# Layer 0 of a four-layer network: VectorE in source order in step one, products a tile later and half of them on POOL, operand blocks of 112 partitions instead of 128

## Chip, cores and metric

The kernel runs on one core of a Trainium2 chip. Its metric is the time on the device of one execution, in microseconds (us); a comparison takes the median over several runs. A profiled execution is one more run, taken with the hardware profiler.

The engines go by the names of the profile: PE is TensorE's matmul and PEld its weight load, DVE is VectorE, ACT ScalarE, POOL GpSimd, SP the sync engine, which here only issues transfers. ACT and POOL issue transfers too, each from its own queue.

## The reference, cut to what matters

Four layers work on an image batch of 8 x 56 x 56 x 192 in float32, each as `x = x + layer(groupnorm(x))`. Only layer 0 is touched by the change:

```python
p = silu(x @ p_w.T + p_b)            # 192 -> 576 channels
q = silu(x @ q_w.T + q_b)
v = silu(x @ v_w.T + v_b)
qv = q * v
a1 = rpe_mlp1(position) * decay      # 111 lags x 576 channels
a2 = rpe_mlp2(position) * decay
o1 = toeplitz(qv along w, a1)        # one 56 x 56 Toeplitz matrix per channel
o2 = toeplitz(qv along h, a2)
out = (p * (o1 + o2)) @ o_w.T + o_b
```

For one channel with the image X (56 rows by 56 columns) this means o1 + o2 = X T1 + T2 X, where T1 and T2 are that channel's Toeplitz matrices. Layer 1 is windowed attention, layer 2 a convolution with four exponential scans, layer 3 a 7 x 7 depthwise convolution and an MLP.

## The kernel before

Activations lie with channels on partitions: a tile of an image is 128 partitions (64 channels twice, once for the upper and once for the lower half of the image) by 3 groups of 64 channels by NH = 1568 pixels. Layer 0 has two stages.

**Step one** (the `with` block from L1321) runs over the 8 images. `layer0_load` (L353) brings an image in from POOL's queue, into one of two buffers. `layer0_in` (L358) takes the statistics of the group norm (four `gn_piece` of three instructions each), finishes them with two small matmuls and a square root, and writes the normed image `xn` (L371), on VectorE throughout. `layer0_qv` (L374) then runs over 14 tiles of two image rows in each half (112 pixels twice). For each half `n` of the 576 channels it makes 24 matmuls into two PSUM tiles (there are four, and they fill PSUM), adds the bias while it empties PSUM (L393, VectorE), takes the Silu in place (L394, ACT) and multiplies q and v into the tile `qv` (L395, VectorE). Both image halves of a tile are then stored by SP to two DRAM tensors: `left`, with an image row per row (L398, one transfer per half), and `right`, transposed, with an image column per row (L403, two transfers per half). Both stores write runs of 256 bytes, 64 channels of one pixel.

Between tiles, in `between[i]`, other work is called: `toeplitz_rows` builds the table of lags in the first image and later the 112 rows of Toeplitz matrices in DRAM, issued by ACT (L296); `build_bias_mask` and `layer1_weights` prepare layer 1; `layer0_in` of the next image is called as a whole after tile 4. The scheduler of the framework orders all engines' instructions itself, by its own estimate of times, and may place an instruction well before its place in the source.

**The mix** (`layer0_mix`, L523) runs over images and nine groups of 64 channels. `layer0_block` (L410) has SP load two operand blocks for a group, `lt` and `rt`, each 128 partitions by 3584 elements: 64 rows of qv and 64 rows of Toeplitz matrix in alternation. Only 56 rows of each are needed. The other eight are zero rows on the Toeplitz side, written in step one (L301, from a row of zeros called `none`), and on the qv side whatever rows follow. There are two buffers for each block (pool `raws`), and the first two pairs are loaded already during step one. `layer0_operand` (L422) copies eight channels of a block at a time into matmul order, `lc` on POOL and `rc` on VectorE and ACT in turn (L425). `layer0_products` (L428) makes one matmul per channel (L433), which sums over the partitions, so over X T1 and T2 X together. The results are copied out, transposed, gated with p and projected (`layer0_gate`); those steps are woven between the products by count. When an image's gate is done its result `x1` is stored (L538, two transfers from 64 partitions each) and a further image loaded (L528), both by SP.

Of the kernel before, what the change touches and what calls it, by code (L numbers as in the profile page):

```python
# [18 lines left out]
NT = H * W  # L19
# [43 lines left out]
NH = NT // 2  # L63
NTH = NH // TT
# [25 lines left out]
def kernel(ctx: ExitStack, tc: tile.TileContext, a: dict, out: bass.AP):  # L90
# [45 lines left out]
    none = dram.tile([QR], F32, name="none")  # L136
    left, right = (dram.tile([(nimg * W + 64) * NSUB, QR], F32, name=n) for n in ("left", "right"))
    qv_row = lambda b, s: (b * NSUB + s) * W
    toep_row = lambda s: nimg * NSUB * W + 64 * s
    x1 = [dram.tile([C, NT], F32, name=f"x1_{b}") for b in range(nimg)]  # L140
# [86 lines left out]
    def toeplitz_rows(psum, pool, rows):  # L227
# [130 lines left out]
    def layer0_in(b, x, pool, psum):  # L358

        sc, sh = scsh[:, 0, b:b + 1], scsh[:, 1, b:b + 1]  # L360
        st = pool.tile([128, 3, NTH, 6], F32, name="gh_st")
        for t in range(NTH):
            gn_piece(st, x, t)
        mv = pool.tile([128, 1, 2], F32, name="gh_mv")
        gn_aggregate(st, mv[:, 0])
        run(gn_finish(mv, sc, sh, pool, psum, "qv"))
        xn = pool.tile([128, 3, NH], F32, name="xn0")
        n = NH if b else TT
        for t in range(NH // n):
            ts = bass.ts(t, n)  # L370
            nc.vector.tensor_scalar(xn[:, :, ts], x[:, :, ts], sc, sh, ALU.mult, ALU.add)  # L371
        return xn

    def layer0_qv(b, xn, pool, psum, w_qv, b_qv, between):  # L374

        lv, rv = (
            z[qv_row(b, 0):qv_row(b, 0) + NSUB * W].rearrange("(s h) (w d) -> s h w d", h=W, d=64) for z in (left, right)
        )
        for i in range(PH):
            qv = pool.tile([2 * W, 2, D1], F32, name="qv", bufs=3)  # L380
            for n in range(2):
                ns = slice(n * D1 // 2, (n + 1) * D1 // 2)
                ps = [psum.tile([2 * W, 2, 512], F32, name=f"qv{s}", tag="qv") for s in range(2)]
                for which in range(2):
                    for j in range(3):
                        for s in range(2):
                            nc.tensor.matmul(  # L387
                                ps[s][:, which, 0:D1 // 2], xn[64 * s:64 * s + 64, j, bass.ts(i, 2 * W)],
                                w_qv[64 * s:64 * s + 64, j, which, ns], start=(j == 0), stop=(j == 2),
                            )  # L390
                for s in range(2):
                    act = pool.tile([2 * W, 2, D1 // 2], F32, name="act", bufs=4)
                    nc.vector.tensor_tensor(act, ps[s][:, :, 0:D1 // 2], b_qv[:, :, ns], ALU.add)  # L393
                    nc.scalar.activation(act, act, AF.Silu)  # L394
                    nc.vector.tensor_tensor(qv[:, s, ns], act[:, 0], act[:, 1], ALU.mult)  # L395
            for s in range(2):
                h0 = H // 2 * s + 2 * i
                nc.sync.dma_start(  # L398
                    lv[:, h0:h0 + 2].rearrange("s h w d -> (h w) s d"),
                    qv[:, s].rearrange("t (s d) -> t s d", d=64),  # L400
                )
                for r in range(2):
                    nc.sync.dma_start(  # L403
                        rv[:, :, h0 + r].rearrange("s w d -> w s d"),
                        qv[r * W:(r + 1) * W, s].rearrange("w (s d) -> w s d", d=64),
                    )
            for step in between[i]:
                step()

    def layer0_block(b, s, raws):  # L410
# [3 lines left out]
        rows_qv, rows_t = qv_row(b, s), toep_row(s)  # L414
        for t, z, even, odd in ((raw[0], left, rows_t, rows_qv), (raw[1], right, rows_qv, rows_t)):
            one = z[even:even + 64]
            nc.sync.dma_start(
                t, bass.AP(one.tensor, one.offset, [[QR, 64], [(odd - even) * QR, 2], [1, QR]]),
            )
        return raw  # L420

    def layer0_operand(copy, raw, name, bufs, d0, nu, pool):  # L422

        c = pool.tile([128, 2, 8, W], F32, name=name, bufs=bufs)
        copy(c[:, 0:nu], raw.rearrange("p (w u d) -> p u d w", u=nu, d=64 // nu)[:, :, d0:d0 + 8])  # L425
# [896 lines left out]
    with ExitStack() as st:  # L1322
# [3 lines left out]
        b_qv = pool.tile([2 * W, 2, D1], F32, name="b_qv", bufs=1)  # L1326
        nc.scalar.dma_start(b_qv.rearrange("p a d -> p (a d)"), a["b_qv"].partition_broadcast(2 * W))
        tz = st.enter_context(tc.tile_pool(reuse_waits="tile", name="tz", bufs=2))
        x = layer0_load(0, pool)
        xn = layer0_in(0, x, pool, psum)  # L1330
# [8 lines left out]
        for b in range(nimg):  # L1339

            between = {i: [lambda i=i: pop(rows, 2 if i % 3 == 1 else 1)] for i in range(PH)}
            if b == 0:
                for i in range(PH):
# [340 lines left out]
```

## Time and profile before

| what | value |
|---|---|
| time, median of 3 runs (lowest to highest) | 5769.45 us (5760.73 to 5771.72) |
| profiled execution, time / span from first to last instruction | 5770.6 us / 5768.8 us |
| start to first L387 matmul | 28.6 us |
| step one, first to last L387 matmul | 28.6 to 847.1 us: PE busy 731.3, VectorE 598.0, ACT 320.4, POOL 42.3 of 818.5 us, DMA share 0.85 |
| mix of layer 0, to its last L433 product | 847.1 to 2052.5 us: PE busy 1083.7, VectorE 652.8, ACT 469.8, POOL 556.7 of 1205.4 us, DMA share 0.67 |
| layers 1 to 3 and what is left of layer 0 | 2052.5 to 5768.8 us |

The busy time of a stretch is the time in which an engine had an instruction of the program under way. The DMA share is the time that packets took on 16 DMA engines, as a part of the stretch. A wait is put down to the instruction that released it last.

### The profile page before, as it was taken

To read this page: it belongs to the slowest core of one execution; us is meant where nothing else is said; L and a number is where in the kernel's file an instruction comes from. 1 tells how busy PE (TensorE), PEld (TensorE's weight loads), DVE (VectorE), ACT (ScalarE), POOL (GpSimd) and SP (SyncE) were. 2 spreads that over 40 slices of the span, in tenths; PEclk is the share of its full clock that TensorE was granted. 3 is DMA by queue.
4 is the path that set the end of the run, shared out by engine and by line. 5 is a ranking of instruction groups with operands and counts; after the bars stand their busy time and mean duration, and the time that the engine had idled before them with its cause. 6 is when DMAs were issued, how large, how long until landed. Compare 5 with 4: busy or idle time off the path is not lost. (4 is left out here: it accounts for less than half of the span.)

```text
span 5768.8 us, 116138 instructions
## 1 busy us (share of the span) xinstructions
PE 5181.2 (90%) x50342; PEld 3376.1 (59%) x50342; DVE 3336.5 (58%) x4710; ACT 2169.1 (38%) x2908; POOL 1420.2 (25%) x1107
## 2 busy tenths in 40 slices
PE   6898998999899979999997989999788798999999
PEld 4568765666666645555554657676344597444444
DVE  5777774555555546566665868888778202433331
ACT  2333443333333423333332004555476400433333
POOL 2100004444444424433342013333101101100100
PEclk8999999999999989999998989999899899999999
DMA  6888986776677633222222866666687598212211
GB/s 179 204 211 216 206 182 258 264 264 258 247 262 264 222 92 82 69 75 76 69 65 76 260 235 218 227 232 209 160 232 215 222 328 295 78 62 77 76 41 26
DMA packets 721922, 1013.94 MB, mean 176 GB/s; under 512 B 486376, under 2 KB 645444, under 8 KB 694644
## 3 DMA queue, kind: packets, MB, share of 16 engines
q1 hardware_dynamic: 706352, 940.12, 52.4%
q0 software_dynamic: 8512, 40.62, 2.1%
q10 hardware_dynamic: 6548, 25.78, 1.4%
q8 instruction: 396, 6.49, 0.5%
q14 instruction: 114, 0.93, 0.0%
HBM read 676.92 MB, written 345.97 MB: 177 GB/s over the span
## 5 line engine op out<-in xcount | busy, mean ns | idle before, releaser
L387 PE MATMUL qv<-w_qv_sb,xn 64*112 64x288 f32 x5376 | 711.3, 421 | 48.6 <-DVE act L393 45.4
L425 POOL COPY lc<-lt 128x896 f32<-128x896 f32 (+1 forms) x320 | 552.5, 1751 | 640.9 <-PE op L433 543.1
L387 PEld LDWEIGHTS qv<-w_qv_sb,xn 64*112 64x112 f32 x5376 | 558.5, 182 | 195.5 <-DVE act L393 58.1
L394 ACT ACTIVATE act<-act 112x576 f32<-112x576 f32 x448 | 300.6, 683 | 466.8 <-DVE act L393 427.4
L433 PE MATMUL op<-rc,lc 128*56 128x56 f32 x9216 | 339.1, 221 | 102.1 <-POOL lc L425 64.9
L433 PEld LDWEIGHTS op<-rc,lc 128*56 128x56 f32 x9216 | 307.8, 135 | 177.9 <-POOL lc L425 103.5
L1289 PE MATMUL ph<-y,w_sb 64*128 64x392 f32 x2304 | 397.7, 497 | 6.5 <-ACT hid L1293 6.5
L1300 PE MATMUL po<-hid,w_sb 128*64 128x392 f32 x2304 | 386.3, 494 | 0.0
L393 DVE TENSOR_TENSOR act<-qv,b_qv 112x576 f32<-112x576 f32 x448 | 320.7, 752 | 92.7 <-PE qv L387 92.4
L1307 DVE TENSOR_TENSOR x<-x,z 128x392 f32<-128x392 f32 x96 | 67.0, 698 | 524.2 <-ACT z L1305 524.2
L425 ACT COPY rc<-rt 128x896 f32<-128x896 f32 (+1 forms) x160 | 256.3, 1606 | 249.7 <-PE op L433 227.2
L805 PE MATMUL qk_ps<-xr,wg 64*96 64x392 f32 x1536 | 334.2, 538 | 1.8 <-DVE xr L752 1.7
L1016 PE MATMUL cv<-zc,wt 128*128 128x224 f32 x1536 | 313.6, 356 | 24.2 <-DMA zc<-pd 24.2
L1016 PEld LDWEIGHTS cv<-zc,wt 128*128 128x128 f32 x1536 | 291.0, 190 | 67.5 <-issue 51.2
L1289 PEld LDWEIGHTS ph<-y,w_sb 64*128 64x128 f32 x2304 | 220.0, 188 | 175.9 <-issue 25.5
L445 PE MATMUL pj<-xn,w_p_sb 64*128 64x392 f32 x1536 | 309.8, 511 | 12.4 <-DVE xn L533 8.2
L1190 PE MATMUL cps<-zc,wt 128*128 128x224 f32 x1536 | 300.2, 356 | 18.2 <-DMA zc<-zd 16.8
L1190 PEld LDWEIGHTS cps<-zc,wt 128*128 128x128 f32 x1536 | 289.6, 189 | 28.7 <-issue 21.3
L466 PE MATMUL y<-pp,w_o_sb 128*64 128x392 f32 x1536 | 285.9, 501 | 4.8 <-DVE x L474 4.1
L459 DVE TENSOR_TENSOR pp<-pp,ot 128x784 f32<-128x784 f32 x128 | 124.2, 970 | 284.8 <-ACT pp L450 272.9
L1300 PEld LDWEIGHTS po<-hid,w_sb 128*64 128x64 f32 x2304 | 162.7, 137 | 213.8 <-issue 213.8
L1031 POOL TENSOR_TENSOR rows<-rows,loc 128x896 f32<-128x896 f32 x96 | 220.8, 2300 | 261.7 <-ACT rows L1027 201.9
(233 smaller groups left out, 8895.1 us busy)
## 6 DMA issues: line engine op xcount, KB each, us to landing
lt<-left SPq DMA_DIRECT2D x72, 1792.0 KB
rt<-right SPq DMA_DIRECT2D x72, 1792.0 KB
left<-qv SPq DMA_DIRECT2D x224, 252.0 KB
right<-qv SPq DMA_DIRECT2D x448, 126.0 KB
wt<-in_band_dram SPq DMA_DIRECT2D x23, 2048.0 KB
wt<-in_band_dram SPq DMA_DIRECT2D x11, 4096.0 KB
zc<-pd SPq DMA_DIRECT2D x187, 232.0 KB
pd<-pt SPq DMA_DIRECT2D x7, 5568.0 KB
```

Source lines behind the costliest of these rows:

```text
L387: nc.tensor.matmul(ps[s][:, which, 0:D1 // 2], xn[64 * s:64 * s + 64, j, bass.ts(i, 2 * W)], w_qv[64 * s:64 * s + 64, j, which, ns], start ...
L393: nc.vector.tensor_tensor(act, ps[s][:, :, 0:D1 // 2], b_qv[:, :, ns], ALU.add)
L394: nc.scalar.activation(act, act, AF.Silu)
L425: copy(c[:, 0:nu], raw.rearrange("p (w u d) -> p u d w", u=nu, d=64 // nu)[:, :, d0:d0 + 8])
L433: nc.tensor.matmul(op[64 * u:64 * u + W, i, :], lc[:, u, i], rc[:, u, i], start=True, stop=True)
L445: nc.tensor.matmul(ps[0:M, s, 0:TT], w_p[64 * s:64 * s + 64, j, d0:d0 + M], xn[64 * s:64 * s + 64, j, ts], start=(j == 0), stop=(j == 2),)
L466: nc.tensor.matmul(y[64 * s:64 * s + 64], w_o[0:M, c, 64 * j:64 * j + 64], pp[0:M, s], start=(c == gated[0][0]), stop=(c == gated[-1][0]),)
L805: nc.tensor.matmul(in_pairs(ps[s]), wg[64 * s:64 * s + 64, j, c0:c0 + HC], in_slots(xr[64 * s:64 * s + 64], (3 * g + j) * GW), start=(j == ...
L1016: nc.tensor.matmul(dst, wt[:, c4 + i, 128 * q:128 * q + 128], zc[:, :, c4 + i, q:q + NPAIR], start=(q == 0), stop=(q == 1),)
L1190: nc.tensor.matmul(dst.rearrange("p (b n) -> p b n", n=NPAIR), wt[:, c4 + i, q * OP:(q + 1) * OP], zc[:, :, c4 + i, q:q + NPAIR], start=(q ...
L1289: nc.tensor.matmul(ps[:, s, 0:TT], w0[64 * s:64 * s + 64, j, m * 128:(m + 1) * 128], y[64 * s:64 * s + 64, j, ts], start=(j == 0), stop=(j ...
L1300: nc.tensor.matmul(ps[64 * s:64 * s + 64], w1[:, m, 64 * j:64 * j + 64], hid[:, m, s], start=(m == 0), stop=(m == 5),)
```

## The change

In step one:

- VectorE's instructions are issued in the order of the source (`manual_schedule` for DVE alone); the other engines stay with the scheduler.
- The first part of the lag table is called before the first image's statistics. `layer0_in` becomes a generator: one statistics piece, or one part of the finish, or two of the four pieces of `xn`, is called after each of tiles 3 to 12 of the image before. The scaling to `xn` goes to POOL for all images but the first.
- The product of q and v is put off by half a tile (`later`): it is issued after the next half's additions. The product of the upper image half stays on VectorE, that of the lower half goes to POOL. The stores follow it; they are the same transfers, in number, size and (for `left`) place.

In the operand blocks: the Toeplitz rows no longer get zero rows behind them, and the row of zeros goes. `right` has its Toeplitz rows first and its qv rows behind. A block is loaded on 112 partitions, 56 rows of qv and 56 of Toeplitz matrix in alternation, now with qv on the even partitions of `lt` and on the odd ones of `rt` (before it was the other way round in both). Copies and products run over 112 partitions.

The diff, cut to its core:

```diff
+QT = [(112 * i, 112) for i in range(14)]
...
-    none = dram.tile([QR], F32, name="none")
+    right_row = lambda b, s: 64 * NSUB + qv_row(b, s)
...
-        zero = pool.tile([128, QR // 128], F32, name="zero", bufs=1)
-        nc.gpsimd.memset(zero, 0.0)
-        nc.scalar.dma_start(none.rearrange("(p n) -> p n", p=128), zero)
-        parts = [z[toep_row(0):].rearrange("(s k) n -> k s n", k=64) for z in (left, right)]
+        parts = [z[at:at + 64 * NSUB].rearrange("(s k) n -> k s n", k=64) for z, at in ((left, toep_row(0)), (right, 0))]
...
-        def zeros(i, k):
-            nc.scalar.dma_start(parts[i][k], none.partition_broadcast(NSUB))
-
-        rows += [lambda i=i, k=k: zeros(i, k) for i in range(2) for k in range(W, 64)]
...
     def layer0_in(b, x, pool, psum):
         sc, sh = scsh[:, 0, b:b + 1], scsh[:, 1, b:b + 1]
         st = pool.tile([128, 3, NTH, 6], F32, name="gh_st")
+        xn = pool.tile([128, 3, NH], F32, name="xn0")
+        yield xn
         for t in range(NTH):
             gn_piece(st, x, t)
+            yield
         mv = pool.tile([128, 1, 2], F32, name="gh_mv")
         gn_aggregate(st, mv[:, 0])
-        run(gn_finish(mv, sc, sh, pool, psum, "qv"))
-        xn = pool.tile([128, 3, NH], F32, name="xn0")
-        n = NH if b else TT
-        for t in range(NH // n):
-            ts = bass.ts(t, n)
-            nc.vector.tensor_scalar(xn[:, :, ts], x[:, :, ts], sc, sh, ALU.mult, ALU.add)
-        return xn
+        for _ in gn_finish(mv, sc, sh, pool, psum, "qv"):
+            yield
+        yield
+        for t in range(NTH):
+            ts = bass.ts(t, TT)
+            eng = nc.gpsimd if b else nc.vector
+            eng.tensor_scalar(xn[:, :, ts], x[:, :, ts], sc, sh, ALU.mult, ALU.add)
+            if t % 2:
+                yield
...
+        def multiply(i, t0, M, n, qv, acts):
+            ns = slice(n * D1 // 2, (n + 1) * D1 // 2)
+            for s in range(2):
+                eng = (nc.vector, nc.gpsimd)[s]
+                eng.tensor_tensor(qv[0:M, s, ns], acts[s][0:M, 0], acts[s][0:M, 1], ALU.mult)
+            for s in range(2 * n):
+                nc.sync.dma_start(
+                    bass.AP(one.tensor, one.offset + 64 * (NH * s + t0), [[64, M], [64 * NT, NSUB], [1, 64]]),
+                    qv[0:M, s].rearrange("t (s d) -> t s d", d=64),
+                )
+                for r in range(2):
+                    nc.sync.dma_start(
+                        rv[:, :, H // 2 * s + 2 * i + r].rearrange("s w d -> w s d"),
+                        qv[r * W:(r + 1) * W, s].rearrange("w (s d) -> w s d", d=64),
+                    )
...
+                acts = [pool.tile([128, 2, D1 // 2], F32, name="act", bufs=4) for _ in range(2)]
                 for s in range(2):
-                    act = pool.tile([2 * W, 2, D1 // 2], F32, name="act", bufs=4)
-                    nc.vector.tensor_tensor(act, ps[s][:, :, 0:D1 // 2], b_qv[:, :, ns], ALU.add)
-                    nc.scalar.activation(act, act, AF.Silu)
-                    nc.vector.tensor_tensor(qv[:, s, ns], act[:, 0], act[:, 1], ALU.mult)
+                    nc.vector.tensor_tensor(acts[s][0:M], ps[s][0:M, :, 0:D1 // 2], b_qv[0:M, :, ns], ALU.add)
+                for s in range(2):
+                    nc.scalar.activation(acts[s][0:M], acts[s][0:M], AF.Silu)
+                if later:
+                    later.pop()()
+                later.append(lambda now=(i, t0, M, n, qv, acts): multiply(*now))
             for step in between[i]:
                 step()
+        later.pop()()
...
     def layer0_block(b, s, raws):
         raw = [raws.tile([128, QR], F32, name=n) for n in ("lt", "rt")]
-        rows_qv, rows_t = qv_row(b, s), toep_row(s)
-        for t, z, even, odd in ((raw[0], left, rows_t, rows_qv), (raw[1], right, rows_qv, rows_t)):
-            one = z[even:even + 64]
-            nc.sync.dma_start(
-                t, bass.AP(one.tensor, one.offset, [[QR, 64], [(odd - even) * QR, 2], [1, QR]]),
-            )
+        x = left[qv_row(b, s):qv_row(b, s) + W]
+        twos = lambda one, delta: bass.AP(one.tensor, one.offset, [[QR, W], [delta * QR, 2], [1, QR]])
+        nc.sync.dma_start(raw[0][0:2 * W], twos(x, toep_row(s) - qv_row(b, s)))
+        rows_t, rows_x = 64 * s, right_row(b, s)
+        nc.sync.dma_start(raw[1][0:2 * W], twos(right[rows_t:rows_t + W], rows_x - rows_t))
         return raw
 
     def layer0_operand(copy, raw, name, bufs, d0, nu, pool):
-        c = pool.tile([128, 2, 8, W], F32, name=name, bufs=bufs)
-        copy(c[:, 0:nu], raw.rearrange("p (w u d) -> p u d w", u=nu, d=64 // nu)[:, :, d0:d0 + 8])
+        c = pool.tile([2 * W, 2, 8, W], F32, name=name, bufs=bufs)
+        copy(c[:, 0:nu], raw[0:2 * W].rearrange("p (w u d) -> p u d w", u=nu, d=64 // nu)[:, :, d0:d0 + 8])
...
         coefs, bias = toeplitz_rows(psum, tz, rows), build_bias_mask(psum, tz, masks)
+        st.enter_context(tc.manual_schedule(engines={mybir.EngineType.DVE}))
+        next(coefs)
+        ahead = layer0_in(0, x, pool, psum)
+        xn = next(ahead)
+        run(ahead)
...
-                between[4].append(lambda: ahead.append(layer0_in(b + 1, x, pool, psum)))
+                ahead = layer0_in(b + 1, x, pool, psum)
+                xn_next = next(ahead)
+                for i in range(3, len(QT) - 1):
+                    between[i].append(lambda: next(ahead, None))
             layer0_qv(b, xn, pool, psum, w_qv, b_qv, between)
-            xn = ahead[0] if ahead else None
+            run(ahead)
+            xn = xn_next
```

More of the change, by code (lines that the diff above doesn't have):

```diff
@@ new lines, in layer0_qv @@
+    def layer0_qv(b, xn, pool, psum, w_qv, b_qv, between):
+        one = left[qv_row(b, 0):qv_row(b, 0) + NSUB * W]
+        at = right_row(b, 0)
+        rv = right[at:at + NSUB * W].rearrange("(s h) (w d) -> s h w d", h=W, d=64)
+        later = []
+        def multiply(i, t0, M, n, qv, acts):
[13 more added lines that the diff above has]
+                    )
+        for i, (t0, M) in enumerate(QT):
+            qv = pool.tile([128, 2, D1], F32, name="qv", bufs=3)
```

32 lines of the change are left out of this document (7 added, 25 removed).

## The prediction

> **What bounds the kernel now.** I read the page's groups first, then windows of 20 us over the first 860 us, the list of waits, and last the timeline of the SP queue and windows over single transfers. The change touches two stages: step one (projections to q and v, up to 847 us) and the mix of layer 0 (854 to 2052 us).
>
> Groups of the page (busy us, mean ns, then idle before and what ended it):
>
> ```profile
> L387 PE MATMUL qv<-w_qv_sb,xn 64*112 64x288 f32 x5376 | 711.3, 421 | 48.6 <-DVE act L393 45.4
> L425 POOL COPY lc<-lt 128x896 f32<-128x896 f32 (+1 forms) x320 | 552.5, 1751 | 640.9 <-PE op L433 543.1
> L393 DVE TENSOR_TENSOR act<-qv,b_qv 112x576 f32<-112x576 f32 x448 | 320.7, 752 | 92.7 <-PE qv L387 92.4
> ```
>
> Windows (busy us and count of PE, PEld, DVE, ACT, POOL, then granted clock, DMA share, GB/s):
>
> ```profile
> 440.00:460.00 20.00, 10.33 (x63) 9.61 (x61) 11.88 (x25) 3.81 (x6) 0.00 (x0) 0.74 0.84 243
> 580.00:600.00 20.00, 20.00 (x168) 20.00 (x167) 15.71 (x28) 8.99 (x14) 0.00 (x0) 1.00 0.93 210
> 740.00:760.00 20.00, 20.00 (x168) 14.88 (x166) 16.00 (x29) 9.43 (x14) 0.00 (x0) 1.00 0.88 181
> ```
>
> Waits before 850 us (total, times, longest):
>
> ```profile
> PE qv L387 <- DVE act L393: 45.4, 15, 9.7
> ...
> DVE gh_st L157 <- DMA x<-in_x_dram: 32.6, 5, 7.7
> ```
>
> The reader is to see that in step one PE runs either full, at 168 matmuls per 20 us (48 make a tile, so 5.7 us a tile), or stands because VectorE is late in emptying PSUM. VectorE is late because statistics of a coming image stand in its queue ahead of their load. The clock drops with the gaps. The first matmuls of the eight images lie at 28.6, 164.8, 286.3, 390.7, 494.0, 592.8, 679.1 and 765.4 us, the last ends at 847.1: lengths 136.2, 121.5, 104.4, 103.3, 98.8, 86.3, 86.3 and 81.7. Against eight of the last, 165 us are lost.
>
> In the mix, SP issues the two operand blocks of a 64-channel group (lt, rt) once the block two before has been copied. Here the fourth image:
>
> ```profile
> 1288.69 0.51 SPq L417 DMA_DIRECT2D lt<-left  x1
> ...
> 1311.81 0.51 SPq L417 DMA_DIRECT2D lt<-left  x1
> ...
> 1319.64 0.51 SPq L417 DMA_DIRECT2D lt<-left  x1
> ...
> 1331.99 0.51 SPq L417 DMA_DIRECT2D lt<-left  x1
> ...
> 1354.59 0.56 SPq L417 DMA_DIRECT2D lt<-left  x1
> ...
> 1376.90 0.51 SPq L417 DMA_DIRECT2D lt<-left  x1
> ...
> 1388.20 0.51 SPq L417 DMA_DIRECT2D lt<-left  x1
> ...
> 1399.15 0.51 SPq L417 DMA_DIRECT2D lt<-left  x1
> ...
> 1438.15 0.51 SPq L417 DMA_DIRECT2D lt<-left  x1
> ```
>
> With one more at 1341.49 the steps are 23.1, 7.8, 12.4, 9.5, 13.1, 22.3, 11.3, 11.0 and 38.9, in sum 149.4 us. Six of nine are under 14 us, and a pair of loads (2 x 1.835 MB at 414 GB/s, below) takes 8.9. So these loads are hidden, but by little. What a load gets depends on its partitions:
>
> ```profile
> 1320.60:1328.60 8.00, 5.69 (x101) 3.52 (x98) 6.20 (x7) 3.23 (x4) 6.62 (x3) 1.00 1.01 414
> 1342.00:1346.00 4.00, 3.97 (x66) 2.65 (x62) 4.00 (x3) 1.65 (x4) 3.59 (x3) 1.00 0.99 204
> ...
> 4196.00:4210.00 14.00, 12.31 (x70) 5.93 (x71) 5.25 (x12) 13.92 (x21) 0.00 (x0) 1.00 0.96 246
> 4309.00:4322.00 13.00, 11.74 (x67) 5.56 (x65) 6.24 (x12) 12.92 (x18) 0.00 (x0) 1.00 0.97 251
> ```
>
> The DMA engines are full in all four. The block loads on 128 partitions move 414 GB/s, the stores of x1 from 64 partitions 204, and the loads of ml in layer 2, the only large ones on **112 partitions**, 246 to 251. Their 43,008 B packets take about 3.06 us in most rounds and 2.15 in the rest, where 26.8 B/ns (14,336 B in the 535 ns of a block packet) would be 1.60; 44,544 B packets of pt on 128 partitions take 1.65.
>
> **The change, part by part.**
>
> Step one, VectorE. Source order takes the early statistics out of the way: one piece of three (3 x 0.554 us) stands between tiles, with its load issued an image before. Products: 448 of 0.461 us become 224. A tile costs VectorE 4 x 0.752 + 2 x 0.461 = 3.9 us instead of 4.9, or 5.6 with a statistics piece, under PE's 5.7. The product now waits for a Silu issued half a tile (2.9 us) before; behind it stand the next additions that free PSUM, and PE waits for those. A Silu takes 0.68 us, so the wait should be empty.
>
> Step one, POOL. A product of 288 elements is not in the trace. POOL's own tensor_tensor rows give 936 ns for 448 elements and 2704 for 1344, a line that gives 0.62 us at 288; its strided row (2300 ns for 896) gives 0.74 in proportion. I take 0.7: 1.4 us of 5.7 a tile. The scaling of x, four pieces of 1176 elements for seven images, is 1.4 us each by POOL's row of 1836 ns for 1568. Both lie under PE. Where the cover is gone: a two-input VectorE product that met a POOL copy at 848.67 us took 3.47 us instead of 0.46. POOL's product starts with its Silu done, VectorE's comes only behind the next two additions, some 2 us later; if they met every time, VectorE would pay 2 x 0.7 more a tile, 5.3 us, still under PE. Queued behind POOL's product are the x load, mask transfers and bmask stores; nobody needs those within an image.
>
> Step one, transfers. Stores are the same in number, size and place, issued half a tile later by SP; qv has three buffers, of which two are in use. Sixteen zero stores of 126 KB go from ACT's queue. Packets fill 0.84 of 850 us over 16 engines, 716 us, so with stores kept step one cannot end much before 740; at full PE speed with Toeplitz rows the share is already 0.93 to 0.96. This floor, not PE, limits the gain.
>
> Sum of step one: images 5 to 7 stay (86.3, 86.3, 81.7). Images 1 to 4, rid of the clustered masks and early statistics, come down to 92, 92, 90, 90: the 86.3 of an image with rows, plus 4 to 6 us for the x load (2352 KB at 414 GB/s is 5.8 us). Image 0 keeps seven tiles with two round trips PE-VectorE-PE for the decay table; at some 2.4 us each that is 33 us over 81.7, 115. Together 733 against 818.5: **-85 us**. Bounds: -30, if the queues fill and images 1 to 4 win half and image 0 nothing; -110 at the DMA floor.
>
> Mix, copies and matmuls. Copies go from 128 to 112 partitions at the same 896 elements in each, matmuls from 128 to 112 rows at the same 56 columns. The additions of 112 x 576 cost 752 ns and of 128 x 768 1545, which follows the elements: zero for both.
>
> Mix, block loads: 144 loads of 112 x 14,336 B (1.606 MB) in place of 128 (1.835 MB). In the DRAM pattern the leading count becomes 56. The right stores of step one have that count too, and their completion packets in the trace come to 14 each, against 16 for left: so two of 16 engines drop out, eight packets each stay, and nothing is won even at the old packet time. Lower bound, by the 414 GB/s row at 14/16 of it: 4.4 us a load, 8.9 a pair, **0 us**. By the nearest row in shape, ml at 250 GB/s: 6.4 and 12.9. By ml's slow rounds (3.06/1.605 = 1.91) in all eight rounds: 8.2 and 16.4, the upper bound. I take 7.9 and 15.7, by the 204 GB/s row between these two: ml's mean holds two fast rounds of seven, and with eight rounds in place of seven the new load need not have any.
>
> A step between issues can't be shorter than its pair. In the image shown the steps of 7.8, 12.4, 9.5, 11.3 and 11.0 become 15.7: 7.9 + 3.3 + 6.2 + 4.4 + 4.7 = 26.5 more. The fifth and sixth (13.1 + 22.3 = 35.4) hold two pairs, the x1 store (2352 KB at 204 GB/s, 11.8) and the x load (5.8): 35.4 at today's 8.9, so this stretch is full already; it becomes 49.0, 13.6 more. That is +40 an image; six images are alike (241), the first, without a store and with steps of 9 to 16, adds 21, the last 38: **+300 us**. With a pair of 12.9 the same sum is 153, with 16.4 it is 336. What is late next: POOL's and VectorE's copies, then PE at L433; everything behind shifts as a whole.
>
> [...]
>
> **Total.** 5770.6 (span 5768.8 plus 1.8 around it; 1.1 over the median of the runs) - 85 + 300 = **5986 us**.
>
> **Rivals.** *The loads keep their rate* (packets of 535 ns on 14 engines): only step one counts, 5770.6 - 85 = 5686, faster. For it: block rows are already spread in alternation, and no load of this split is in the trace. Against it: both rows under 128 partitions are far slower. It decides as long as a pair stays under about 11 us: by the steps above a pair of 11 costs 3.2, 1.5 and, in the fifth and sixth together, 4.2 us an image, some 70 in all, and the gain is nearly gone. *Step one is bound by its stores and wins nothing*, loads unchanged: the early statistics go, but SP's right stores take 7.8 us a pair when full (439 us), qv's third buffer fills and PE waits for POOL's product instead: 5770, with -30 at best. Against it, at 580 us PE, rows and stores run together at full speed.
>
> **How the numbers follow.** Slow loads: 0.68, own range 5830 to 6060 (153 to 370 with -85 to -110). Loads at their rate with the gain: 0.26, 5655 to 5750. Nothing won: 0.06, half of it within 0.2%, which is about what a measurement of this kernel can tell. The range 5690 to 6060 leaves out half of the second case and a little on top, under 0.2. Faster 0.27, same 0.03, slower 0.70.
>
> **What would show it.** Step one: last L387 matmul near 762 us, windows with 168 matmuls from the second image on, waits of PE for L393 gone. Mix: DMA share near 1 with about 200 GB/s, lc and rc waiting for lt and rt, steps of 15 to 17 us, the stage 1490 us long instead of 1198. If GB/s in a block load stays at 360 or more, I am wrong on the sign.

## The result, and the profile after

| | before | after |
|---|---|---|
| median (lowest to highest) of 4 runs each, us | 5767.2 (5760.7 to 5771.7) | 6036.8 (6015.6 to 6042.5) |
| profiled execution: time / span, us | 5770.6 / 5768.8 | 6042.5 / 6040.7 |
| step one, from the span's start to the last projection matmul | 847.1 | 813.5 |
| mix of layer 0, from there to the last product | 1205.7 | 1508.2 |
| all behind it | 3716.1 | 3719.0 |

The changed kernel takes 1.046 times as long (95% interval 1.043 to 1.049). In the profiled executions step one won 33.6 us, the mix lost 302.5 and the rest moved by 3.

The page after: clock, DMA share and traffic in 40 slices of 151 us (the mix is the sixth to fifteenth), then the groups that answer to those of before.

```profile
PEclk9999978878889888999999898999899999899999
DMA  6999987787777783222222386677667598321210
GB/s 176 220 222 214 192 208 162 174 203 184 179 164 182 192 188 88 69 75 78 66 78 62 97 266 229 230 236 232 179 189 212 176 332 316 125 75 55 93 41 25
...
L434 POOL COPY lc<-lt 112x896 f32<-112x896 f32 (+1 forms) x320 | 519.9, 1642 | 972.9 <-PE op L442 751.0
L404 PE MATMUL qv<-w_qv_sb,xn 64*112 64x288 f32 x5376 | 705.0, 416 | 25.8 <-DVE act L410 21.6
...
L410 DVE TENSOR_TENSOR act<-qv,b_qv 112x576 f32<-112x576 f32 x448 | 318.0, 751 | 211.6 <-PE qv L404 186.7
```

In the mix the DMA engines are mostly seven or eight tenths busy and yet move only 162 to 208 GB/s. Busy engines with little traffic are the sign to look for: each packet takes longer (a row of a block load 1041 ns at the median here, 535 before). VectorE's idle time in step one has turned round: it waited 92 us for PE before, now 187, and PE's waits for the PSUM it empties fell from 45.4 us to 21.6.

Two windows of 10 us inside the third image's mix, where little but block loads runs, with the columns as before (busy us and count of PE, PEld, DVE, ACT, POOL, clock, DMA share, GB/s):

```profile
1300.00:1310.00 10.00, 7.49 (x77) 4.68 (x77) 3.09 (x4) 3.19 (x3) 3.29 (x2) 0.94 0.89 199
...
1320.00:1330.00 10.00, 10.00 (x94) 6.98 (x92) 3.27 (x4) 4.33 (x4) 2.95 (x2) 0.50 0.89 199
```

A share of 0.89 over 16 engines is 14.2 engines, as if fourteen carried the load and two stood by. The completion packets of 4 bytes, which the prediction counted for the stores, say the same: between 1290 and 1340 us there are 84 of them to 692 rows, 13.6 to a load of 112. At 199 GB/s a load of 1.606 MB takes 8.1 us and a pair 16.1. The 14,336-byte packets of the whole stage have a median of 1041 ns (535 before) and a mean of 1013 (584 before).

The list of waits of the stage (total, times, longest), and SP's issues of lt in the same image as before (other transfers between them left out):

```profile
POOL lc L434 <- DMA lt<-left: 216.0, 46, 10.1
...
DVE rc L434 <- DMA rt<-right: 174.1, 33, 12.9
ACT rc L434 <- DMA rt<-right: 152.8, 31, 9.9
PE op L442 <- POOL lc L434: 147.3, 68, 7.3
```

```profile
1376.75 0.79 SPq L426 DMA_DIRECT2D lt<-left  x1
1399.87 0.78 SPq L426 DMA_DIRECT2D lt<-left  x1
1408.55 0.79 SPq L426 DMA_DIRECT2D lt<-left  x1
1426.52 0.79 SPq L426 DMA_DIRECT2D lt<-left  x1
1443.98 0.82 SPq L426 DMA_DIRECT2D lt<-left  x1
1458.35 0.79 SPq L426 DMA_DIRECT2D lt<-left  x1
1486.65 0.78 SPq L426 DMA_DIRECT2D lt<-left  x1
1503.12 0.78 SPq L426 DMA_DIRECT2D lt<-left  x1
1519.02 0.78 SPq L426 DMA_DIRECT2D lt<-left  x1
1564.27 0.78 SPq L426 DMA_DIRECT2D lt<-left  x1
```

The steps are 23.1, 8.7, 18.0, 17.5, 14.4, 28.3, 16.5, 15.9 and 45.2 us: 187.5 for the image against 149.4 before. Before, lc waited 62.7 us for lt in 14 places; now 216 us in 46. The copies wait for data, and PE for the copies. PE loses clock with it: 0.85 granted over the mix, 0.97 before.

Step one by the waits of PE, from 28 us to its end. Before (the 45.4 us for emptied PSUM stand in the prediction) and after:

```profile
PE cps L286 <- DVE co L279: 17.8, 7, 9.0
PE gh_v L176 <- DVE gh_d L184: 11.6, 7, 2.4
PE wmean L665 <- DVE act L393: 6.3, 1, 6.3
PE bp L325 <- DVE act L393: 5.2, 1, 5.2
```

```profile
PE gh_m L177 <- DVE gh_mv L161: 29.4, 7, 11.5
PE qv L404 <- DVE act L410: 21.6, 10, 3.7
PE qv L404 <- DVE xn L369: 3.2, 1, 3.2
PE aps L278 <- DVE act L410: 2.3, 8, 0.5
```

All of PE's waits come to 90 us before and 61 after, and the projection matmuls themselves, at a slightly better clock (0.93 and 0.95 granted), to 711 and 705 us: 35 us, nearly all of the 37 by which the way from the first to the last projection matmul got shorter (the first one comes 3.3 us later). The waits for emptied PSUM halved (45.4 to 21.6) and those of the decay table, all its steps together, fell from 18.7 to 5.6. In their place stands a new one: PE waits 29.4 us at the matmul of the GroupNorm mean, because VectorE, in source order, reaches the aggregation that feeds it later than PE does. The longest of these waits, 11.5 us, stands in the first image; there VectorE itself waits for ScalarE, as the experiments show.

### The profile page after: what moved, and what is told of

Its sections match the earlier page's. It is cut to its first block, busy times and chain, and to the rows that moved or that the text cites. A ratio compares the mean times of both kernels' runs of the same rounds, so it can differ in the third digit from the quotient of the medians.

```text
span 6040.7 us, 116146 instructions
## 1 busy us (share of the span) xinstructions
PE 5313.6 (88%) x50342; PEld 3442.5 (57%) x50342; DVE 3195.8 (53%) x4479; ACT 2161.2 (36%) x2908; POOL 1616.5 (27%) x1358
## 5 line engine op out<-in xcount | busy, mean ns | idle before, releaser
L434 POOL COPY lc<-lt 112x896 f32<-112x896 f32 (+1 forms) x320 | 519.9, 1642 | 972.9 <-PE op L442 751.0
L404 PE MATMUL qv<-w_qv_sb,xn 64*112 64x288 f32 x5376 | 705.0, 416 | 25.8 <-DVE act L410 21.6
L404 PEld LDWEIGHTS qv<-w_qv_sb,xn 64*112 64x112 f32 x5376 | 532.7, 179 | 188.2 <-DVE act L410 34.9
L442 PE MATMUL op<-rc,lc 112*56 112x56 f32 x9216 | 397.7, 245 | 257.1 <-POOL lc L434 147.3
L442 PEld LDWEIGHTS op<-rc,lc 112*56 112x56 f32 x9216 | 363.6, 158 | 341.5 <-POOL lc L434 186.3
L434 ACT COPY rc<-rt 112x896 f32<-112x896 f32 (+1 forms) x160 | 254.4, 1591 | 478.1 <-PE op L442 316.7
L454 PE MATMUL pj<-xn,w_p_sb 64*128 64x392 f32 x1536 | 347.3, 561 | 13.1 <-DVE xn L542 9.1
L384 POOL TENSOR_TENSOR qv<-act 112x288 f32<-112x288 f32 x224 | 189.1, 846 | 503.5 <-ACT act L412 350.3
L1199 PE MATMUL cps<-zc,wt 128*128 128x224 f32 x1536 | 299.9, 356 | 18.4 <-DMA zc<-zd 16.6
```

Of the source, the lines that this page charges most:

```text
L404: nc.tensor.matmul(ps[s][0:M, which, 0:D1 // 2], xn[64 * s:64 * s + 64, j, t0:t0 + M], w_qv[64 * s:64 * s + 64, j, which, ns], start=(j == ...
L434: copy(c[:, 0:nu], raw[0:2 * W].rearrange("p (w u d) -> p u d w", u=nu, d=64 // nu)[:, :, d0:d0 + 8])
L442: nc.tensor.matmul(op[64 * u:64 * u + W, i, :], lc[:, u, i], rc[:, u, i], start=True, stop=True)
L454: nc.tensor.matmul(ps[0:M, s, 0:TT], w_p[64 * s:64 * s + 64, j, d0:d0 + M], xn[64 * s:64 * s + 64, j, ts], start=(j == 0), stop=(j == 2),)
L1199: nc.tensor.matmul(dst.rearrange("p (b n) -> p b n", n=NPAIR), wt[:, c4 + i, q * OP:(q + 1) * OP], zc[:, :, c4 + i, q:q + NPAIR], start=(q ...
```

## The experiments

Twelve kernels ran, beside the kernel before on the same chip each time. Stage lengths are those of one profiled execution each, which lay between 13 us under the median (e1) and 12 over it (v1), so a few us of stage length say little. "Before" was between 5763 and 5771 us throughout.

| kernel | time, us | ratio to before (95%) | step one | mix |
|---|---|---|---|---|
| e1 128 partitions loaded | 5732.4 | 0.9948 (0.9932 to 0.9965) | 803.5 | 1215.3 |
| e2 before, 112 loaded | 6058.2 | 1.0513 (1.0494 to 1.0531) | 846.1 | 1489.5 |
| e3 seven rows an engine | 5879.1 | 1.0206 (1.0186 to 1.0227) | 806.5 | 1371.3 |
| e4 Toeplitz rows spread | 5739.8 | 0.9953 (0.9937 to 0.9968) | 808.9 | 1213.0 |
| s1 large right stores | 5725.6 | 0.9939 (0.9917 to 0.9961) | 803.7 | 1212.6 |
| s2 products on VectorE | 5743.7 | 0.9965 (0.9952 to 0.9978) | 814.2 | 1208.1 |
| s3 rows issued by SP | 5738.9 | 0.9963 (0.9950 to 0.9976) | 801.4 | 1225.3 |
| s6 products at once | 5737.6 | 0.9961 (0.9947 to 0.9975) | 817.9 | 1205.4 |
| v1 rows by four | 5742.0 | 0.9962 (0.9948 to 0.9976) | 826.0 | 1211.7 |
| v2 mean a step later | 5723.8 | 0.9918 (0.9901 to 0.9935) | 803.7 | 1211.3 |
| v3 v1 and v2 | 5731.7 | 0.9943 (0.9928 to 0.9959) | 806.6 | 1213.6 |
| p1 rows on POOL's queue | 5725.8 | 0.9931 (0.9910 to 0.9952) | 797.1 | 1210.0 |

### Where the 300 us come from

**e1.** The changed kernel with its loads on 128 partitions again and everything else kept.

```
-    toep_row = lambda s: nimg * NSUB * W + 64 * s
-    right_row = lambda b, s: 64 * NSUB + qv_row(b, s)
+    qv_row = lambda b, s: (b * NSUB + s + NSUB) * W
+    toep_row = lambda s: W * s
+    right_row = qv_row
...
-        twos = lambda one, delta: bass.AP(one.tensor, one.offset, [[QR, W], [delta * QR, 2], [1, QR]])
-        nc.sync.dma_start(raw[0][0:2 * W], twos(x, toep_row(s) - qv_row(b, s)))
+        twos = lambda one, delta: bass.AP(one.tensor, one.offset, [[QR, 64], [delta * QR, 2], [1, QR]])
+        nc.sync.dma_start(raw[0], twos(x, toep_row(s) - qv_row(b, s)))
```

> The changed kernel, but each load of lt and rt fills all 128 partitions again (64 rows of each tensor, alternating; the Toeplitz rows lie 56 to a slice ahead of the x rows, so the eight extra rows are rows of the next slice, and eight tail rows are written once). Operands and matmuls stay on 112 partitions. Theory (112-partition loads send 8 rows through each of 14 engines and each row takes twice as long): rows of 14336 bytes go back from about 1040 ns to about 535 ns, the mix from 1508 us to about 1205 us, the whole to about 6037 - 302 = 5735 us, with step one's 34 us kept. Rival (the copies and matmuls on 112 partitions, or the new order, slow the mix): rows may get faster but the whole stays above 5950 us.

**e2.** The other way round: the kernel before, with this one thing of the change.

```
-            one = z[even:even + 64]
+            one = z[even:even + W]
             nc.sync.dma_start(
-                t, bass.AP(one.tensor, one.offset, [[QR, 64], [(odd - even) * QR, 2], [1, QR]]),
+                t[0:2 * W], bass.AP(one.tensor, one.offset, [[QR, W], [(odd - even) * QR, 2], [1, QR]]),
             )
...
-        c = pool.tile([128, 2, 8, W], F32, name=name, bufs=bufs)
+        c = pool.tile([2 * W, 2, 8, W], F32, name=name, bufs=bufs)
```

> The kernel before with one thing of the change: the loads of lt and rt read 56 rows of each tensor instead of 64 and the operands have 112 partitions; step one, its zero rows and its order are as before. Theory: rows take about 1040 ns, the mix is about 300 us longer, the whole about 5767 + 302 = 6070 us. Rival (the loss is due to the new place or order of the rows in memory, or to step one's new order): about 5767 us.

**e3.** Loads of 112 partitions again, but of 112 successive rows. The rows no longer alternate, so the values are not the reference's.

```
-        twos = lambda one, delta: bass.AP(one.tensor, one.offset, [[QR, W], [delta * QR, 2], [1, QR]])
+        twos = lambda one, delta: bass.AP(one.tensor, one.offset, [[QR, 2 * W], [1, QR]])
```

> The changed kernel with each load of lt and rt reading 112 successive rows of one tensor (so the halves no longer alternate and the wrong rows are multiplied), which gives 16 engines seven rows each. Theory A (it is 14 engines with eight rows each, not 112 partitions as such): a row comes near the rate of the 112-partition load of a later layer (250 GB/s), 12.9 us a pair, the whole about 6037 - 150 = 5885 us, perhaps down to 5735. Theory B (any load that ends at partition 112 is slow): about 6037 us.

All three fell where the theory put them: 5732 (5735 expected), 6058 (6070) and 5879 (5885). One window of each in a stretch of block loads, e1, e2 and e3 in that order (e3's four windows from 1200 to 1240 us, some with other transfers, show 215 to 296 GB/s):

```profile
1320.00:1330.00 10.00, 9.84 (x102) 6.23 (x98) 3.17 (x4) 2.36 (x3) 3.40 (x2) 1.00 1.00 426
```

```profile
1350.00:1360.00 10.00, 7.10 (x83) 5.20 (x81) 3.27 (x4) 4.11 (x4) 3.46 (x2) 0.66 0.90 200
```

```profile
1210.00:1220.00 10.00, 10.00 (x130) 6.44 (x127) 3.38 (x5) 1.81 (x3) 0.00 (x0) 1.00 1.00 240
```

With 128 partitions all engines are busy and move 426 GB/s, also with the changed step one and layout in memory; the row packets are back at a median of 535 ns, and lc waits 71 us for lt. With 112 in the kernel before the picture of the changed kernel appears, 200 GB/s at a share of 0.90, and rows of 1038 ns. So the loss is that of the loads: taking them back wins 293 us of the mix (e1), and they alone cost 284 (e2). The order of the halves and the operands on 112 partitions have at most some 10 us in it. e3 splits the loss: 16 busy engines (a share of 1.00), seven of the 112 rows to each on average, give 240 GB/s, near the 246 to 251 of the ml loads from which the prediction had its price of 12.9 us a pair, and the mix is 1371 us, half-way. Its rows are still slow, 936 ns at the median. So two engines standing by is a part of the loss (in the mix e3 has 2828 completion packets where the changed kernel has 2542, two more for each of 140 loads), and packets that take nearly twice as long on a full set of engines is another. How much each is worth is not settled, since e3 changed the order of the rows along with their split.

Which engine carried which row is not in the trace. The slow time is that of most rows, not of a few: the means are 1013 ns in the changed kernel and 1004 in e2. Of the 692 rows between 1290 and 1340 us of the changed kernel none took under 888 ns and 99 in 100 took over 900; in its whole mix 86 in 100 did. So why a row takes nearly twice as long in a load of 112 partitions stays open.

### Where the missing 50 us of step one are

e1 keeps step one's edits without the slow loads, so the rest was tried on it. Its step one is 803.5 us; the last image, with no rows, masks or x load, takes 82.

**e4**, **s1**: is it the DMA engines? Their share is 0.89 to 0.98 in images 1 to 5 (images are counted from 0 here, as in the prediction). e4 spreads the Toeplitz rows, which go to nine engines (nine completion packets to a transfer of nine rows; which nine is not in the trace, and that they are always the first was the author's assumption), over all 16 (e4 has some 160 packets to a transfer, 144 of them data and so some 16 of completion); s1 stores right in large pieces, in another order, so that its values are not the reference's.

```
+            src = coef[i][:, 55 - w0:111 - w0].rearrange("s l d -> s (l d)")
...
-                parts[i][w0], coef[i][:, 55 - w0:111 - w0].rearrange("s l d -> s (l d)")
+                parts[i][w0].rearrange("s (k n) -> k s n", k=16), src.rearrange("s (k n) -> k s n", k=16)
```

> As the kernel with all 128 partitions loaded, and the Toeplitz rows are stored in 16 pieces of 896 bytes a row, so that they go over 16 engines instead of nine. Theory (step one is now set by the store traffic of the first nine DMA engines, about 778 of its 813 us): about 30 us less in step one, the whole about 5705 us. Rival (step one is set by the chain of PE, VectorE, ScalarE and POOL): the same as with all 128 partitions loaded, about 5735 us.

```
                     nc.sync.dma_start(
-                        rv[:, :, H // 2 * s + 2 * i + r].rearrange("s w d -> w s d"),
-                        qv[r * W:(r + 1) * W, s].rearrange("w (s d) -> w s d", d=64),
+                        bass.AP(right.tensor, right[at:at + 1].offset + D1 * (NH * s + t0 + r * W), [[D1, W], [1, D1]]),
+                        qv[r * W:(r + 1) * W, s],
                     )
```

> The kernel with all 128 partitions loaded (5732 us, step one 803 us), with the stores of right written as 56 rows of 2304 bytes instead of 504 pieces of 256 bytes: the same bytes in an eighteenth less than half the packets of step one, in another order in memory (so the right operand's rows are not the reference's). Theory S (the stores' packets set step one): an image's DMA work falls by about 17 us over 16 engines (28952 packets of 19.5 ns make 35 us, 3217 of about 90 ns make 18 us), images 1 to 4 go from 91 to 107 us to about 86 to 95, step one to about 765 us, the whole to about 5695 us. Rival (step one is set by the chain of PE, VectorE, ScalarE and POOL): about 5732 us.

(The count in this expectation is misput: a ninth of right's packets is left, which makes an eighteenth more than half of all.) Windows by image, e1 and then s1; images 2, 3 and 4:

```profile
247.00:354.00 107.00, 98.17 (x742) 82.73 (x744) 67.04 (x123) 40.91 (x61) 35.48 (x42) 0.94 0.89 214
354.00:457.00 103.00, 92.58 (x682) 68.26 (x680) 61.01 (x110) 37.20 (x57) 33.30 (x37) 0.95 0.95 234
457.00:551.00 94.00, 87.56 (x676) 62.10 (x674) 60.31 (x110) 39.57 (x61) 32.75 (x37) 0.98 0.96 225
```

```profile
247.00:354.00 107.00, 96.91 (x743) 77.59 (x744) 66.96 (x122) 41.59 (x63) 36.49 (x43) 0.95 0.80 224
354.00:457.00 103.00, 91.70 (x683) 78.02 (x681) 60.96 (x111) 39.19 (x59) 32.92 (x37) 0.93 0.83 228
457.00:551.00 94.00, 86.98 (x686) 62.69 (x684) 60.66 (x111) 39.57 (x59) 32.66 (x37) 0.98 0.83 224
```

e4 missed its 30 us: step one is 5 us longer, not shorter, as its rival had it. In s1 the mean share of images 1 to 5 falls from 0.95 to 0.83 and every image is as long as in e1, to 2 us; its rival was right too. Step one isn't set by how long its packets keep the engines busy, and the floor of 740 us in the prediction, made from that share, is not what stopped the gain.

**s2**, **s6**: the other two parts of the change, each undone alone.

```
-                eng = (nc.vector, nc.gpsimd)[s]
+                eng = nc.vector
```

> The kernel with all 128 partitions loaded, both products of a tile on VectorE instead of one on POOL. Theory P (POOL's 846 ns product and its waits hold the act tiles): step one shorter by 10 us or more. Rival 1 (the half on POOL is what won 44 us against the kernel before): step one 15 to 40 us longer, the whole 5750 to 5770 us. Rival 2 (neither matters, because VectorE has about 78 us of work in an image of 82 to 107): within 10 us of 5732 us.

```
-                if later:
-                    later.pop()()
-                later.append(lambda now=(i, t0, M, n, qv, acts): multiply(*now))
+                multiply(i, t0, M, n, qv, acts)
```

> The kernel with all 128 partitions loaded, each product in its own tile's turn instead of a tile later. VectorE, now in source order, then waits for the Silu of each tile (0.68 us and the hand-over, 224 tile halves, of which PE's four buffers hide a part). Theory (putting off the products is what VectorE's source order needs): step one 20 to 60 us longer, the whole 5750 to 5790 us. Rival (it is hidden): within 8 us of 5732 us.

Without POOL's half step one is 10.7 us longer in the profile, without the delay 14.4; in the whole times neither can be told from e1 (0.9965 and 0.9961 against 0.9948). The losses of 15 to 40 and of 20 to 60 us were too high. With 28 products of 0.56 us (e1) instead of 56 of 0.45 (before), VectorE saves some 10 us an image, but it had the time. If the two add up, 25 of e1's 43.6 us are theirs and some 18 are left for the third part, source order with GroupNorm's pieces spread over the tiles; that fits the tiles that took 18.7 and 18.4 us before in images 3 and 4 and 9.2 and 9.3 after, but it was not tried alone.

**s3**, **v1**, **p1**: are ScalarE and SP held at the Toeplitz rows? A row is issued on ScalarE's queue, in front of a Silu. In e1's trace the transfers of SP and ScalarE wait for and raise the same eight semaphores in turn (POOL's have eight others), so a row waits there for the store eight places ahead of it to land.

```
-            nc.scalar.dma_start(
+            nc.sync.dma_start(
                 parts[i][w0], coef[i][:, 55 - w0:111 - w0].rearrange("s l d -> s (l d)")
```

> The kernel with all 128 partitions loaded, the Toeplitz rows issued by SP instead of ScalarE's queue. Theory (ScalarE is held at the issue of rows while the DMA engines are full; its Silu waits on DMA for about 100 us in step one): step one 10 to 25 us shorter, the whole about 5710 to 5720 us. Rival (those waits hide behind the stores or PE): within 8 us of 5732 us.

```
+            one = coef[i][:, 55 - w0:111 - w0]
...
-                parts[i][w0], coef[i][:, 55 - w0:111 - w0].rearrange("s l d -> s (l d)")
+                parts[i][:, w0:w0 + 4], bass.AP(one.tensor, one.offset, [[111 * 64, NSUB], [-64, 4], [1, QR]])
...
-            between = {i: [lambda i=i: pop(rows, 2 if i % 3 == 1 else 1)] for i in range(len(QT))}
+            between = {i: [lambda i=i: pop(rows, 1 if i % 3 == 1 else 0)] for i in range(len(QT))}
```

> The kernel with all 128 partitions loaded (5732 us, step one 803 us), four Toeplitz rows to a transfer: 28 issues on ScalarE's queue instead of 112. Its program has each transfer of SP's and ScalarE's queues wait for the one eight places before it, whichever queue that was, to land; so a row on ScalarE waits for a store of SP's, and the Silu behind it waits too. Theory: ScalarE's waits on DMA in step one fall from about 115 us to under 50, the long last steps of images 2, 3 and 4 (11.5, 8.8 and 11.0 us against 5.8) go, step one is 10 to 25 us shorter, the whole about 5715 us. Rival (those waits cost PE nothing, or the larger transfers hold the stores as long): within 8 us of 5732 us.

```
-            nc.scalar.dma_start(
+            nc.gpsimd.dma_start(
                 parts[i][w0], coef[i][:, 55 - w0:111 - w0].rearrange("s l d -> s (l d)")
```

> The kernel with all 128 partitions loaded, the Toeplitz rows issued on POOL's queue, whose transfers have eight semaphores of their own, so that neither ScalarE's Silus nor SP's stores stand in one line with the rows. 112 issues of about 0.6 us are 67 us more work for POOL, which has 270 us in step one's 771. Theory H (the rows' place in the line of the stores is what step one's images 1 to 4 still lose, 91.5, 106.9, 102.6 and 94.4 us against 85.3 without rows): images 1, 3 and 4 fall to 86 to 90 us, step one to about 770 us, the whole to about 5700 us, the best of all. Rival T (the rows' traffic itself holds up the stores, whoever issues it): step one 795 to 810 us, within 10 us of 5732 us. Rival P (POOL is held at the rows as ScalarE was, and its products with it): step one over 815 us.

e1 shows ScalarE held, and p1 shows what becomes of it (waits in step one; e1, then p1):

```profile
POOL qv L386 <- DMA right<-qv: 102.5, 33, 8.0
ACT act L414 <- DMA right<-qv: 57.2, 17, 10.0
POOL qv L386 <- DMA left<-qv: 55.9, 18, 9.2
...
ACT act L414 <- DMA left<-qv: 43.4, 8, 9.1
...
ACT act L414 <- DMA coef<-ct: 15.2, 1, 15.2
```

```profile
POOL qv L386 <- DMA right<-qv: 185.9, 48, 9.6
...
DVE qv L386 <- DMA right<-qv: 43.7, 20, 7.4
```

In p1 ScalarE's waits for stores have gone from the head of the list, and products wait for them instead: the three buffers of qv are all in use and a product waits for the stores of three tiles before. One piece was won for good. In image 0 of e1 ScalarE stands 15.2 us at the first row, until the coefficient table has landed; p1's image 0 takes 115.9 us instead of 123.4, the 115 of the prediction. Images 1 to 4 take 391 us in place of 395; of 1, 3 and 4, which were to fall to 86 to 90 each, only image 1 did (88.7), so rival T, with step one at 795 to 810, was right. s3 does the same more sharply: ScalarE's waits for stores fall to 3 us, and those of the products rise to 394, from 166 in e1. v1's larger transfers made them longer too (image 1 takes 119 us). s3 was to win 10 to 25 us of step one and won 2, v1 as much and lost 23. So the hold at the rows is real, and taking it away wins little: the wait moves to the products.

**v2**, **v3**: the new wait at the GroupNorm mean.

```
         gn_aggregate(st, mv[:, 0])
+        yield
         for _ in gn_finish(mv, sc, sh, pool, psum, "qv"):
```

> The kernel with all 128 partitions loaded, the GroupNorm mean's matmul (gh_m) one step of 112 tokens after the aggregation that feeds it instead of in the same step. PE now waits there 25 us in seven images, and the two steps behind run at 6.3 us instead of 5.8. Theory: step 7 of each image falls from 8.5 to about 5.9 us and the two behind it to 5.8, 7 x (2.7 + 1.0) = 26 us, the whole about 5706 us. Rival (PE runs ahead of VectorE and would have waited for something else): within 8 us of 5732 us.

> Both of these edits on the kernel with all 128 partitions loaded. If they hit separate waits, as the theories have it, the gains add: step one about 760 us, the whole about 5690 us, 1.3% below the kernel before. Rival (the stores set step one's length and one gain takes the other's place): no better than the better of the two alone.

PE's waits in e1 and in v2:

```profile
PE gh_m L177 <- DVE gh_mv L161: 25.4, 7, 11.5
PE qv L406 <- DVE act L412: 21.2, 12, 3.1
```

```profile
PE qv L407 <- DVE act L413: 26.7, 15, 3.7
PE gh_m L177 <- DVE act L413: 6.8, 1, 6.8
```

The wait went as expected (the eighth tile of images 4 to 6 takes 5.8 us instead of 8.5 to 8.9), and step one is as long as it was. The timelines of VectorE and POOL in image 5 of v2 tell why:

```profile
608.75 1.42 DVE L413 TENSOR_TENSOR act<-qv,b_qv 112x576 f32<-112x576 f32 x2
610.09 6.28 DVE L387 TENSOR_TENSOR qv<-act 112x288 f32<-112x288 f32 x1
616.29 1.41 DVE L413 TENSOR_TENSOR act<-qv,b_qv 112x576 f32<-112x576 f32 x2
```

```profile
610.08 3.92 POOL L372 TENSOR_SCALAR xn<-x,scsh 128x1176 f32<-128x1176 f32 x3
613.98 0.78 POOL L387 TENSOR_TENSOR qv<-act 112x288 f32<-112x288 f32 x1
614.75 1.31 POOL L372 TENSOR_SCALAR xn<-x,scsh 128x1176 f32<-128x1176 f32 x1
```

Scaling x starts a tile later with the mean and now bunches on POOL, and one product of VectorE, 0.44 us otherwise, is under way for all of it, 6.28 us. The next additions come that much later, and PE, which waits for them, stands 3.7 us until 617 us. The wait costs more than itself: in the 4.9 us behind it the granted clock was 0.65 and only 24 matmuls ran, and that tile takes 12.0 us. Image 6, where POOL issues no masks beside, has the same with a product of 6.47 us and a tile of 10.8. Five of the seven images whose x POOL scales hold a product of 4.1 to 6.5 us. In sum PE's waits fell by 10 us from e1 to v2 (57 to 47), and the projection matmuls are busy 10.6 us longer (700.0 and 710.6).

VectorE's products that met work on POOL took 29 us more in v2's step one than at their median, 15 in e1 and 13 in the changed kernel, where no single one took over 1.52. In p1 and s3 it is 24 and 26 us, with single products of up to 4.2 and 3.6; whether that is what kept these two from winning more is not shown.

v2 has the lowest median of all, 5723.8 us, but its profiled step one is e1's to 0.2 us, so what its whole time won, if anything, is not explained by it. v3 is no sum: 806.6 us, no better than v2, as its rival had it.

The versions with 128 partitions loaded beat both kernels: e1, p1 and v2 take 0.995, 0.993 and 0.992 of the time before and 0.95 of the time after. Which of them is best isn't settled.

## Why the prediction was right, and where it was off

The prediction was 5986 us, 51 under the median; sign, cause and stage were right.

- **Mix, block loads, +300 us:** measured +302.5. The price taken from the 204 GB/s row of 64 partitions, 7.9 us a load, was measured at 199 GB/s and 8.1. The split over 14 engines shows in the share of 0.89 (so the share was not near 1, as the signs had it) and in the completion packets, 13.6 to a load. e2 and e1 show that this part makes nearly all of the loss; the rival in which the loads keep their rate is out. That the price came out so close is partly luck: the row was that of a store on other partitions, picked between two bounds, and the upper one, 8.2, lies as near. The upper bound itself came from a misreading: in the two windows quoted, ml's packets don't take 3.06 us in most rounds but anything from 2.0 to 3.3, with a median of 2.8. For the 370 us behind the upper end of the range no run shows a source; the mix grew by 302.5 in the changed kernel and by 284 in e2.
- **The sum over the images, +40, +21 and +38:** near in total by errors that cancel. By the last product of each image, the first grew by 41 us where 21 were put, the six alike by 37 on average where 40 were put, and the last by 38. Nor does the image shown grow where the sum says. "A step between issues can't be shorter than its pair" is wrong: the second step took 8.7 us, not 15.7, with a pair at 16.1. The fifth and sixth together grew by 7.3 us instead of 13.6, and the last, left at 38.9, grew by 6.3. The total of the image, +38 for +40, was right all the same.
- **Copies and matmuls on 112 partitions, zero:** right; e1 has them too, and its mix is 10 us longer than before, with lc copies of 1739 ns (1751 before) and matmuls of 223 (221). The rows quoted for it don't show it: from 576 to 768 elements 752 ns became 1545. A better pair is 112 x 576 at 752 ns and 128 x 576 at 746. In the changed kernel the matmuls take 245 ns, at the lower clock.
- **Step one, -85 us:** this term was mis-sized; it measured -34 in the changed kernel and -44 in e1. The changed kernel's images took 122.1, 90.1, 105.5, 108.5, 93.2, 93.3, 87.0 and 81.9 us, where 115, 92, 92, 90, 90, 86.3, 86.3 and 81.7 were put. Image 1 and the last two were right. Image 0 lost 7 us at a wait that the prediction's sum did not have, ScalarE's for the coefficient table (p1 takes it away and reaches 115.9). Images 2 and 3 lost 32 together, images 4 and 5 ten, the later start three. "Rid of the clustered masks and early statistics" was true, but the sum let no new wait stand in their place; the mean's matmul, 29 us in all, is one (11.5 of them are the wait in image 0). Taking it away alone wins nothing in step one, since another stands right behind it: VectorE's product held beside POOL's scaling of x (v2).
- **"With stores kept step one cannot end much before 740":** not what binds. s1 lowers the share of step one from 0.89 to 0.77 and its length stays at 803.7 us.
- **POOL's product at 0.7 us, x scaled in 1.4 us a piece:** 0.85 and 1.49. VectorE's own half rose from 0.46 to 0.51 us a product: 26 of its products took 0.6 to 1.5 us. The fear of 3.47 us where both meet was right in kind. But the prediction priced only the meeting with POOL's product; the scaling of x, which it moved to POOL in the same breath, is the longer neighbour, with products of 3.6 us in s3, 4.2 in p1 and 6.5 in v2.

What stays open: why images 2 and 3, beside which Toeplitz rows, weights and masks move, take 194 to 215 us together in all these versions, where 182 were put. Store packets, the spread of the rows, their number to a transfer, the queue that issues them, POOL's half and the delayed product were each changed alone and moved step one by -6 to +23 us. Common to the versions shown is that products wait for stores to land and that VectorE's products lengthen beside POOL's scaling (in the changed kernel to 0.92 us, the median of the 12 that lay mostly beside it, from 0.45 alone); that these make the loss is not shown. Not tried: the scaling of x on an engine other than POOL, source order alone, more buffers for qv, and more semaphores for the two queues.

## What to carry to other kernels

How a load's rows fall on partitions and engines was part of its speed here: dropping the 16 idle partitions of 128 cut the bytes by an eighth and halved the rate (426 to 199 GB/s), so padding rows may be what keeps a transfer fast. Before a load is reshaped, look in the trace for any transfer of the new shape and price the step between issues by it, not by its bytes. And when stalls of one stage are removed, add the engines' times in their new order, and look which instructions it puts side by side: here the next wait stood a few microseconds behind the one taken away.

## What the runs showed of the hardware that was not expected

Sixteen busy engines with seven rows each on average were no remedy: packets of 14,336 B still took 936 ns at the median in e3, against 535 in e1, where the loads fill 128 partitions. And nearly halving the number of store packets in step one, at the same bytes, lowered the DMA share from about 0.95 to 0.83 without making an image shorter: a share near one was not a bound there. And a VectorE product, 0.44 us alone, lasted 6.28 and 6.47 us beside a run of POOL's scaling, while the additions out of PSUM showed nothing of it: in the changed kernel the 30 that lay mostly beside POOL's scaling took 0.75 us at the median and 0.76 at most, as alone.
